# SBUF pools that wait tile by tile, a token quantizer on VectorE alone, and key tiles filled by ScalarE, in an eleven-block perceiver kernel

## The chip, the cores and the metric

The kernel runs on one core of one Trainium2 chip. A core has five engines with a queue of instructions each: TensorE (PE in the profile, with its weight loads as PEld), VectorE (DVE), ScalarE (ACT), GpSimd (POOL) and SyncE (SP), which here issues the DMA transfers. They run side by side and wait for one another through semaphores. The metric is the device time of one execution in microseconds (us); the median of several runs is compared.

## What is computed

The reference is a perceiver-like network of four layers on 2 batches of 256 tokens with 256 features (512 tokens in all), with a context of 4096 rows for each batch. Each layer has a cross attention to the context, a self attention and a feed-forward block. The block that most of the change lies in is layer 0's feed-forward, in which both products take quantized operands:

```
def act_quant(x):
    scale = 127.0 / clip(max(abs(x), axis=-1), 1e-05)
    return clip(round(x * scale), -128, 127) / scale
def weight_quant(w):
    scale = 1.0 / clip(mean(abs(w)), 1e-05)
    return clip(round(w * scale), -1, 1) / scale
def bit_linear(x, w):
    xq = x + stop_gradient(act_quant(x) - x)
    wq = w + stop_gradient(weight_quant(w) - w)
    return einsum('bsd,hd->bsh', xq, wq)
# block: layernorm -> bit_linear(w1) to 1024 features -> depthwise convolution
#        over 3 tokens -> silu -> bit_linear(w2) back to 256 -> + x
```

Each token has its own scale, the largest magnitude of its features. The value that enters the product is x + (quantized - x), in that order of operations.

## The kernel before

Activations stand in SBUF with features on the partitions: x is a tile of [128, 2, 512] (two halves of the features by 512 tokens), float32. The program is eleven blocks, one after the other: l0_xattn, l0_attn, l0_ffn together with l1_xattn, l1_attn, l1_ffn, l2_xattn, l2_attn, l2_ffn, l3_xattn, l3_attn, l3_ffn. In the profiled execution L0's cross attention fills about 40 to 700 us, L0_attn's attention 767 to 848, L0_ffn 850 to 954, L1's cross attention 970 to 1635.

A scheduler orders the instructions of most blocks; inside manual_schedule the named engines keep the order in which the program is written. Both large cross attentions (class ContextAttention) are written out by hand for PE, VectorE and ScalarE. The order of all other instructions is the same before and after the change.

Memory comes from pools that are opened and closed with the blocks. A pool that is opened over the bytes of closed ones must wait for those who used them. The argument reuse_waits says how: with "pool" (the default) all its tiles wait for every user of the closed pools whose bytes the new pool lands on; with "tile" each tile waits only for the users of earlier tiles on its own bytes. The pools of PSUM and of the small temporary tiles (banks, stage) have "tile" already; the SBUF pools of the blocks have the default.

L0_ffn runs inside the set-up of L1's cross attention: context_attention opens its pools xa and xa_ctx, the constructor of ContextAttention has POOL clear two xa_top tiles (L780) and fill fourteen key tiles xa_k of 128x512 with ones (L783), and then calls l0_ffn with the generator begin(3), which projects three sets of keys. l0_ffn advances it one step at a time (run(between, 1)), so PE's k_ps products (L1001) stand between its own. SP copies masks (key_masks) and dense keys into the filled key tiles.

The steps of L0_ffn, in order:

- Before it, L0_attn quantizes the weights: w1 on VectorE, w2 on POOL (quantize_weights, L522 to L526, two parts of 128x1024). Then x is complete (L312).
- norm: mean (PE), xc (VectorE L232), sq (ScalarE L233), var (PE), a table load and rstd (ScalarE L249, VectorE L250), rstd_ps (PE), h (VectorE L281).
- to_tokens transposes h into tok_ps (PE L563); two copies into hn, one on ScalarE and one on VectorE (L219).
- quantize_tokens(hn): the largest magnitude (L533), four operations on 128x4 for scale and inverse (L534 to L537), and for each of 4 groups of 128 tokens five operations: times the scale and rounded (L522), lower bound (L523), upper bound and rescaled (L524), minus src (L525), plus src (L526).
- from_tokens transposes back (feat_ps, PE L574), copies (L219), and w1's products follow (proj), the convolution (ScalarE L1237, VectorE L1240) and silu (ScalarE L1243).
- by_token for each of the 4 groups: eight transposes to hid_tok (PE L1254), a copy to tok (ScalarE L1258), quantize_tokens of 128x1024, with L525 on POOL and the rest on VectorE.
- For each group: eight transposes to feat_ps, two copies to hidq (L219, dealt to ScalarE and VectorE by the scheduler), and w2's products into l0f_out (PE, 16 products in 32 instructions).

Other places that the change touches: the value tiles xv of the cross attentions, set by eleven POOL memsets of 128x1148 (L1038) at their start, beside which VectorE makes the queries xa_q (L816, L818 or L820); the table loads ahead of the first exponential of a self attention (ScalarE L368 in L0_attn and L2_attn, L1439 in L1_attn and L3_attn); in L3_attn the memset of sa_v (POOL L1317) and the band mask (POOL L1848 and L1851, cast by VectorE L1863).

Of the kernel before, what the change touches and what calls it, by code (L numbers as in the profile page):

```python
# [19 lines left out]
F32 = mybir.dt.float32  # L20
# [3 lines left out]
ALU = mybir.AluOpType  # L24
# [46 lines left out]
class Net:  # L71
# [385 lines left out]
    def attend_to_context(self, a, x, q_bias, wq, wo, alive):  # L457
        tc = self.tc
        with self.stage():
            norm = self.center(self.halves(x))  # L460
            if not a.begun:
                a.beginning = a.begin(2)
                run(a.beginning, 1)
            a.take_queries(norm, wq, q_bias, alive)
        with (
            self.banks(mm=1, sc=3, acc=1),
            tc.tile_pool(name="xa_v", bufs=1) as vpool,
            tc.tile_pool(name="xa_p", bufs=1) as ppool,
            tc.tile_pool(name="focus", bufs=2) as fpool,
        ):  # L470
            a.attend(vpool, ppool, fpool)
        with self.stage():
            return a.give_back(x, wo)

    def context_constants(self):
# [8 lines left out]
        self.key_masks = self.tc.dram_tile([2, NR, KC], F32, name="key_masks")  # L484
        with self.banks(), self.tc.tile_pool(name="mask", bufs=1) as tmp:
            mi = tmp.tile([NR, KC], I32, name="mask_i", tag="mask_i")
# [29 lines left out]

    def quantize(self, work, out, src, scale, inverse, low, high, first, second, third):


        n = src.shape[-1]  # L520
        t = work.tile([P, 1024], F32, tag="quant", name="quant", bufs=2)[:, :n]
        first.tensor_scalar(t, src, scale, MAGIC, ALU.mult, ALU.add)  # L522
        first.tensor_scalar(t, t, MAGIC, low, ALU.subtract, ALU.max)  # L523
        first.tensor_scalar(t, t, high, inverse, ALU.min, ALU.mult)  # L524
        second.tensor_tensor(t, t, src, ALU.subtract)  # L525
        third.tensor_tensor(out, t, src, ALU.add)  # L526

    def quantize_tokens(self, work, out, src, rows, between=None):

# [6 lines left out]
        nc.vector.tensor_scalar_mul(scale, scale, 127.0)  # L536
        nc.vector.reciprocal(inverse, scale)  # L537
        for r in range(rows):
            of = scale[:, r : r + 1], inverse[:, r : r + 1]
            self.quantize(work, out[:, r, :], src[:, r, :], *of, -128.0, 127.0, nc.vector, between or nc.vector, nc.vector)  # L540

    def quantize_weights(self, work, w, total, n, engine):
# [9 lines left out]
        for at in range(0, 2048, 1024):  # L552
            part = w[:, at : at + 1024]
            self.quantize(work, part, part, scale, inverse, -1.0, 1.0, engine, engine, engine)

# [11 lines left out]

    def from_tokens(self, outs, src, n):

        for m in range(0, n, 4):  # L570
            k = min(4, n - m)
            ps = self.mm("feat_ps")
            for i in range(k):
                self.nc.tensor.transpose(ps[:, i * P : (i + 1) * P], src[:, (m + i) * P : (m + i + 1) * P], self.ident)  # L574
            self.copy(outs(m, k), ps[:, : k * P].rearrange("p (k t) -> p k t", k=k))
# [185 lines left out]
class ContextAttention:  # L761
# [11 lines left out]
    def __init__(self, net, layer, big, cpool, keys, values):  # L773
# [7 lines left out]
        self.key_tiles = [tile([P, KC], f"k{i}") for i in range(self.KEY_TILES)]  # L781
        for t in self.key_tiles:
            self.nc.gpsimd.memset(t, 1.0)  # L783
        self.begun, self.beginning = 0, iter(())
# [363 lines left out]
def l0_attn(net, x):  # L1148
# [8 lines left out]
    NCH = 8  # L1157
    with tc.tile_pool(name="l0a", bufs=1) as big, tc.tile_pool(name="l0a_w", bufs=2) as work:
        cos, sin = net.vec("rope_cos", big), net.vec("rope_sin", big)
# [58 lines left out]
def l0_ffn(net, x, between):  # L1218
# [4 lines left out]
    NCH = 8  # L1223
    with tc.tile_pool(name="l0f", bufs=1) as big, tc.tile_pool(name="l0f_w", bufs=2) as work:
# [26 lines left out]
        def by_token(t):  # L1251
# [36 lines left out]
def small_attention(net, x, wq, wk, wv, wo, scale, qb=None, kb=None, vb=None, ob=None, window=None):  # L1288

    by_program = {mybir.EngineType.PE, mybir.EngineType.DVE, mybir.EngineType.Activation}  # L1290
    with net.tc.manual_schedule(engines=by_program):
        with net.tc.tile_pool(name="sa", bufs=1) as big, net.tc.tile_pool(name="sa_w", bufs=1) as work:
            a = SmallAttention(net, big, work, scale, vb, window)
# [180 lines left out]
def l1_ffn(net, x):  # L1474
# [7 lines left out]
    hc = [h[:, d, :] for d in range(ND)]  # L1482
    with tc.tile_pool(name="l1f", bufs=1) as big, tc.tile_pool(name="l1f_w", bufs=2) as work:
        tile3 = lambda name: big.tile([P, NT, E], F32, name=name, tag=name)
# [83 lines left out]
def l2_xattn(net, x):  # L1568
# [5 lines left out]
    with (  # L1574
        tc.manual_schedule(engines={mybir.EngineType.PE}),
        tc.tile_pool(name="l2x", bufs=1) as big,
        tc.tile_pool(name="l2x_t", bufs=5) as cpool,
        tc.tile_pool(name="l2x_n", bufs=4) as npool,
    ):
# [100 lines left out]
def l2_attn(net, x):  # L1680
# [10 lines left out]
    NCH = 8  # L1691
    with tc.tile_pool(name="l2a", bufs=1) as big, tc.tile_pool(name="l2a_w", bufs=2) as work:
        mask = mask_tile(net, big, "causal", (1, 0))
# [46 lines left out]
def l2_ffn(net, x):  # L1740
# [8 lines left out]
    h = net.norm(x)  # L1749
    with tc.tile_pool(name="l2f", bufs=1) as big:  # L1750
        mixed = [big.tile([P, ND, T], F32, name=f"mix{i}", tag=f"mix{i}") for i in range(2)]
# [24 lines left out]
def l3_xattn(net, x):  # L1776
# [3 lines left out]
    net.measure(norm)  # L1780
    with tc.tile_pool(name="l3x", bufs=1) as big, tc.tile_pool(name="l3x_w", bufs=2) as work:

# [94 lines left out]
def l3_ffn(net, x):  # L1877
    nc, tc = net.nc, net.tc
    E, NCH, HC = 64, 4, 2
    y = net.norm(x)  # L1880
    with tc.tile_pool(name="l3f", bufs=1) as big, tc.tile_pool(name="l3f_w", bufs=2) as work:
        mask = mask_tile(net, big, "window", (1, 0), (-1, P))
# [319 lines left out]
```

## Time and profile before

| | before |
|---|---|
| median of 3 runs | 2561.95 us (2557.09 to 2562.78) |
| the profiled execution's own time | 2563.84 us |
| its span, first to last instruction | 2562.1 us |
| mean granted TensorE clock | 0.953 |
| busy PE / DVE / ACT / POOL | 2343.6 / 1558.8 / 1054.6 / 355.6 us |

The profile is of one execution. A row of its timeline gives the start (us from the span's start), the busy time, the engine, the line of the program, the operation, the tiles written and read with their shapes, and how many instructions are put together; in brackets stands how long the engine had been idle and what released it. L219 and L180 are the lines of helpers (a copy, a product), so these rows are told apart by their tiles. The chain that ended last follows the execution back from its last instruction, at each step to what released it. In the stretches of L0_ffn the engines were busy as follows:

| stretch, us | PE | DVE | ACT | POOL | granted clock |
|---|---|---|---|---|---|
| 838 to 876 | 23.00 | 11.64 | 3.36 | 35.51 | 0.79 |
| 876 to 886 | 0.00 | 9.62 | 0.59 | 6.92 | 0.50 |
| 886 to 913 | 21.40 | 15.17 | 13.77 | 0.00 | 0.85 |
| 913 to 955 | 31.37 | 27.67 | 8.38 | 9.49 | 0.84 |

### The profile page before, as it was taken

What the parts mean: (1) busy time and instruction counts of PE and PEld (TensorE: products, weight loads), DVE (VectorE), ACT (ScalarE), POOL (GpSimd) and SP (SyncE); (2) the same over time, 40 slices, a digit from 0 to 9 for tenths busy, and PEclk for the clock granted to TensorE, in tenths of its full rate; (3) what the DMA queues carried; (4) which work ended last, traced back from release to release, by engine and by line L of the source; (5) the groups of instructions that cost most, each with busy time, mean ns of one, the idle gap of its engine ahead of it and who ended that gap; (6) DMA issues with size and microseconds to landing.
All of it is one profiled execution on the core that took longest, in us unless ns stands there. A gap on an engine that the chain in (4) does not pass through costs nothing.

```text
span 2562.1 us, 42559 instructions
## 1 busy us (share of the span) xinstructions
PE 2343.6 (91%) x17006; PEld 1247.1 (49%) x17014; DVE 1558.8 (61%) x2702; ACT 1054.6 (41%) x1830; POOL 355.6 (14%) x523
## 2 busy tenths in 40 slices
PE   7999999999998579999999999989999996789998
PEld 3454545544544354544555544554448453345453
DVE  4968897779546468888878878243331254335252
ACT  2455555555616132555555555431131252223141
POOL 3000010000034612100011000000020031003030
PEclk9999999999989789999999999988999897898989
DMA  5432223231010133232222220202222100000100
GB/s 191 137 97 80 93 88 94 71 107 43 10 55 17 47 107 108 91 95 95 94 88 82 83 76 26 81 14 61 87 89 88 42 18 14 33 21 12 56 12 21
DMA packets 97797, 174.40 MB, mean 68 GB/s; under 512 B 15120, under 2 KB 63888, under 8 KB 96704
## 3 DMA queue, kind: packets, MB, share of 16 engines
q1 hardware_dynamic: 97600, 171.68, 20.7%
q8 instruction: 135, 2.21, 0.4%
q14 instruction: 62, 0.51, 0.1%
HBM read 154.25 MB, written 0.59 MB: 60 GB/s over the span
## 4 chain that ended last, share of the span: by engine, by line
PE 79%; DVE 10%; ACT 5%; issue 3%; POOL 2%; DMA 1%; SPq 0%; ACTq 0%; DVEq 0%; POOLq 0%
PE s L1080 11%; PE s L1104 10%; PE attn_acc L1128 9%; PE v_ps L180 6%; PE proj L180 6%; PE k_ps L1001 4%; DVE mx L1088 3%; PE kc_sum L180 2%; PE expert L180 2%; PE s L180 2%; PE c_acc L1666 2%; PE f_ps L180 2%; PE ffn_ps L180 2%; PE s L1402 2%; PE o L411 1%
## 5 line engine op out<-in xcount | busy, mean ns | idle before, releaser
L1088 DVE TENSOR_REDUCE mx<-s 128x2 f32<-128x1024 f32 x512 | 603.5, 1220 | 206.3 <-PE s L1080 203.6
L1114 ACT ACTIVATE p<-s 128x1024 f32<-128x1024 f32 x512 | 496.3, 1021 | 237.9 <-PE s L1104 235.8
L1104 PE MATMUL s<-xa_q,xa_k 32*128 32x256 f32 x4096 | 339.0, 403 | 22.9 <-DVE mx L1088 20.8
L1080 PE MATMUL s<-xa_k,xa_q 32*128 32x512 f32 x2048 | 345.3, 639 | 7.6 <-ACT p L1114 3.6
L1104 PEld LDWEIGHTS s<-xa_q,xa_k 32*128 32x128 f32 x4096 | 211.8, 184 | 160.5 <-issue 98.5
L1128 PE MATMUL attn_acc<-p,xv 128*32 128x256 f32 x4096 | 277.1, 387 | 0.9 <-ACT p L1114 0.9
L1080 PEld LDWEIGHTS s<-xa_k,xa_q 32*128 32x128 f32 x2048 | 116.4, 183 | 128.9 <-issue 58.7
L654 DVE TENSOR_TENSOR ge<-fy 128x960 bf16<-128x960 f32 (+14 forms) x240 | 172.9, 720 | 6.2
L1128 PEld LDWEIGHTS attn_acc<-p,xv 128*32 128x32 f32 x4096 | 107.5, 109 | 132.2 <-issue 85.5
L611 POOL TENSOR_TENSOR fy<-fy,low 128x256 f32<-128x256 f32 x64 | 50.4, 787 | 793.1 <-ACT low L610 793.1
L656 DVE TENSOR_TENSOR rank<-rank,ge 128x960 bf16<-128x960 bf16 (+14 forms) x240 | 111.4, 464 | 6.0
L658 DVE TENSOR_TENSOR rank<-rank,ge 128x960 bf16<-128x960 bf16 (+14 forms) x240 | 105.6, 440 | 2.7
L387 POOL TENSOR_SCALAR p<-p,r 128x128 f32<-128x128 f32 (+1 forms) x192 | 82.7, 444 | 140.2 <-DVE r L383 80.0
L1048 ACT COPY xv<-v_ps 128x512 f32<-128x512 f32 x64 | 37.6, 588 | 142.8 <-PE v_ps L180 133.0
L368 ACT ACTIVATE p<-p,top 128x256 f32<-128x256 f32 (+1 forms) x128 | 57.1, 447 | 42.7 <-DVE top L356 40.2
L180 PE MATMUL f_ps<-f_wk,f_ctx 128*128 128x256 f32 x256 | 70.0, 401 | 1.2 <-ACT low L610 1.2
L1001 PE MATMUL k_ps<-ctx_k,w_L0x_wq 128*64 128x512 f32 x256 | 65.1, 615 | 2.6 <-DMA ctx_k<-in_ctxT 2.2
L1666 PE MATMUL c_acc<-pT,ctx_n 128*128 128x256 f32 x256 | 63.1, 392 | 4.2 <-ACT pT L1639 3.0
L180 PEld LDWEIGHTS f_ps<-f_wk,f_ctx 128*128 128x128 f32 x256 | 44.1, 189 | 46.8 <-issue 27.3
L233 ACT ACTIVATE sq<-xc 128x512 f32<-128x512 f32 x24 | 14.7, 630 | 125.8 <-DVE xc L232 125.8
L180 PE MATMUL v_ps<-w_L0x_wv,ctx_v 128*128 128x256 f32 x256 | 63.8, 392 | 0.8 <-ACT k_dense L1014 0.8
L180 PE MATMUL kc_sum<-f_tok,fy 128*128 128x257 f32 x256 | 64.2, 393 | 0.0
(458 smaller groups left out, 3365.1 us busy)
## 6 DMA issues: line engine op xcount, KB each, us to landing
ctx_k<-in_ctxT SPq DMA_DIRECT2D x128, 512.0 KB
ctx_v<-in_ctxT SPq DMA_DIRECT2D x64, 256.0 KB
xa_k<-k_dense SPq DMA_DIRECT2D x512, 32.0 KB
f_ctx<-in_ctxT SPq DMA_DIRECT2D x32, 256.0 KB
f_tok<-in_ctx SPq DMA_DIRECT2D x16, 512.0 KB
ctxT<-in_ctxT SPq DMA_DIRECT2D x16, 512.0 KB
ctx_n<-in_ctx SPq DMA_DIRECT2D x16, 512.0 KB
xa_k<-key_masks SPq DMA_DIRECT2D x128, 8.0 KB
```

Of the source, the lines that this page charges most:

```text
L180: self.nc.tensor.matmul(out, lhsT=lhsT, rhs=rhs, start=i == 0, stop=i == len(pairs) - 1)
L387: nc.gpsimd.tensor_scalar(p[:, j, :nk], p[:, j, :nk], r[:, j : j + 1], 1.0, ALU.mult, ALU.mult)
L654: nc.vector.tensor_tensor(ge[:, :, :n], w[:, :, :n], w[:, :, P - n :], ALU.is_ge)
L656: nc.vector.tensor_tensor(rank[:, :, P - n :], rank[:, :, P - n :], ge[:, :, :n], ALU.add)
L658: nc.vector.tensor_tensor(rank[:, :, :n], rank[:, :, :n], ge[:, :, :n], ALU.subtract)
L1001: nc.tensor.matmul(ps[i * HR : (i + 1) * HR, :], lhsT=self.wk[:, d, c * HR : (c + 1) * HR], rhs=ctx[:, d, :], start=d == 0, stop=d == ND - 1,)
L1080: nc.tensor.matmul(pairs[i // 2][:, i % 2, :], lhsT=self.q[u][rows, qt * P : (qt + 1) * P], rhs=k[rows, :], start=True, stop=True,)
L1088: nc.vector.tensor_reduce(mx[:, qt, 2 * i : 2 * i + 2, kc], sc, AX.X, ALU.max)
L1104: nc.tensor.matmul(pairs[i // 2][:, i % 2, kk * S : (kk + 1) * S], lhsT=k[rows, at], rhs=self.q[u][rows, :], start=True, stop=True,)
L1114: nc.scalar.activation(p, sc, AF.Exp, scale=DH**-0.5)
L1128: nc.tensor.matmul(self.acc[i * HP : (i + 1) * HP, :S], lhsT=v[:, 2 * k2 + kk, at : at + HP], rhs=ps[i // 2][:, i % 2, kk * S : (kk + 1) * S],
L1666: nc.tensor.matmul(accs[m], lhsT=of[:, (k + i) % (KC // P), m * P : (m + 1) * P], rhs=pT[:, i, :], start=k + i == 0, stop=k + i == KT - 1,)
```

## The change

It has three parts.

1. Every SBUF pool of the blocks gets reuse_waits="tile" (on sixteen lines; one of them is shown).
2. The token quantizer runs on VectorE alone. For the 1024-wide tokens of L0_ffn it stops ahead of the last addition and returns the difference (quant); from_tokens then makes the sum on PE: two products with the identity, of tok and of the difference, accumulate into feat_ps in place of one transpose. The quant tile has four buffers for two. Both hidq copies that VectorE did go to ScalarE.
3. L1's fourteen key tiles are filled by ScalarE, which copies a column of ones, as a first step of begin; l0_ffn runs that step behind the quantization of hn in program order, and the scheduler puts five of the copies ahead of sq, one between the two sq, one ahead of rstd's table load and seven ahead of the hn copy. L0's key tiles stay with POOL.

Counted in instructions: POOL loses 14 memsets and 4 subtractions; ScalarE gains 14 + 2 copies; VectorE gains 4 subtractions and loses 4 additions and 2 copies; PE gets 64 products for 32 transposes.

The waits that change with the pools, as far as the prediction speaks of them: the hn copies no longer wait for the end of w2's quantization on POOL, the second L522 of the tokens waits for it instead; most xv memsets wait for sq and PE's last query projection, no longer for VectorE's last L816, and only the tenth waits for VectorE; the table loads at L368 and at L1497 (L1_ffn) no longer wait for VectorE's data, while the one at L1439 in L3_attn waits for PE's s; the memset of sa_v in L3_attn waits for an earlier copy on VectorE (yT) in place of the last y.

```diff
-        with tc.tile_pool(name="xa", bufs=1) as big, tc.tile_pool(name="xa_ctx", bufs=2) as cpool:
+        with tc.tile_pool(name="xa", bufs=1, reuse_waits="tile") as big, tc.tile_pool(name="xa_ctx", bufs=2, reuse_waits="tile") as cpool:
...
-    def quantize(self, work, out, src, scale, inverse, low, high, first, second, third):
+    def quantize(self, work, out, src, scale, inverse, low, high, engine):
...
-        t = work.tile([P, 1024], F32, tag="quant", name="quant", bufs=2)[:, :n]
-        first.tensor_scalar(t, src, scale, MAGIC, ALU.mult, ALU.add)
-        first.tensor_scalar(t, t, MAGIC, low, ALU.subtract, ALU.max)
-        first.tensor_scalar(t, t, high, inverse, ALU.min, ALU.mult)
-        second.tensor_tensor(t, t, src, ALU.subtract)
-        third.tensor_tensor(out, t, src, ALU.add)
+        t = work.tile([P, 1024], F32, tag="quant", name="quant", bufs=4)[:, :n]
+        engine.tensor_scalar(t, src, scale, MAGIC, ALU.mult, ALU.add)
+        engine.tensor_scalar(t, t, MAGIC, low, ALU.subtract, ALU.max)
+        engine.tensor_scalar(t, t, high, inverse, ALU.min, ALU.mult)
+        engine.tensor_tensor(t, t, src, ALU.subtract)
+        if out is not None:
+            engine.tensor_tensor(out, t, src, ALU.add)
+        return t
...
-    def from_tokens(self, outs, src, n):
+    def from_tokens(self, outs, src, n, more=None):
...
-                self.nc.tensor.transpose(ps[:, i * P : (i + 1) * P], src[:, (m + i) * P : (m + i + 1) * P], self.ident)
+                at, to = slice((m + i) * P, (m + i + 1) * P), ps[:, i * P : (i + 1) * P]
+                if more is None:
+                    self.nc.tensor.transpose(to, src[:, at], self.ident)
+                else:
+                    self.matmuls(to, [(of[:, at], self.ident) for of in (src, more)])
...
-        for t in self.key_tiles:
-            self.nc.gpsimd.memset(t, 1.0)
+        if layer == 0:
+            for t in self.key_tiles:
+                self.nc.gpsimd.memset(t, 1.0)
...
         self.begun = n
+        if self.layer > 0:
+            for t in self.key_tiles:
+                self.nc.scalar.copy(t, self.net.ones[:, 0:1].to_broadcast([P, KC]))
+            yield
         for j in range(n):
...
         net.quantize_tokens(work, hn, hn, NT)
+        run(between, 1)
         hq = big.tile([P, ND, T], F32, name="hq", tag="hq")
...
-            net.quantize_tokens(work, tok, tok, 1, nc.gpsimd)
-            toks.append(tok)
+            toks.append((tok[:, 0, :], *net.quantize_tokens(work, None, tok, 1)))
...
-            net.from_tokens(lambda m, k: hidq[:, m : m + k, at], toks[t][:, 0, :], NCH)
+            tok, more = toks[t]
+            net.from_tokens(lambda m, k: hidq[:, m : m + k, at], tok, NCH, more)
```

More of the change, by code (lines that the diff above doesn't have):

```diff
@@ L466, in attend_to_context @@
             self.banks(mm=1, sc=3, acc=1),
-            tc.tile_pool(name="xa_v", bufs=1) as vpool,
-            tc.tile_pool(name="xa_p", bufs=1) as ppool,
-            tc.tile_pool(name="focus", bufs=2) as fpool,
+            tc.tile_pool(name="xa_v", bufs=1, reuse_waits="tile") as vpool,
+            tc.tile_pool(name="xa_p", bufs=1, reuse_waits="tile") as ppool,
+            tc.tile_pool(name="focus", bufs=2, reuse_waits="tile") as fpool,
         ):
@@ L484, in context_constants @@
         self.key_masks = self.tc.dram_tile([2, NR, KC], F32, name="key_masks")
-        with self.banks(), self.tc.tile_pool(name="mask", bufs=1) as tmp:
+        with self.banks(), self.tc.tile_pool(name="mask", bufs=1, reuse_waits="tile") as tmp:
             mi = tmp.tile([NR, KC], I32, name="mask_i", tag="mask_i")
@@ L514, in context_constants, with quantize_tokens @@
             nc.vector.tensor_scalar_min(self.alive, ps[:, :NB], 1.0)
-    def quantize(self, work, out, src, scale, inverse, low, high, first, second, third):
+    def quantize(self, work, out, src, scale, inverse, low, high, engine):
         n = src.shape[-1]
-        t = work.tile([P, 1024], F32, tag="quant", name="quant", bufs=2)[:, :n]
-        first.tensor_scalar(t, src, scale, MAGIC, ALU.mult, ALU.add)
-        first.tensor_scalar(t, t, MAGIC, low, ALU.subtract, ALU.max)
-        first.tensor_scalar(t, t, high, inverse, ALU.min, ALU.mult)
-        second.tensor_tensor(t, t, src, ALU.subtract)
-        third.tensor_tensor(out, t, src, ALU.add)
-    def quantize_tokens(self, work, out, src, rows, between=None):
+        t = work.tile([P, 1024], F32, tag="quant", name="quant", bufs=4)[:, :n]
[6 more added lines that the diff above has]
+        return t
+    def quantize_tokens(self, work, out, src, rows):
         nc = self.nc
@@ L537, in quantize_tokens @@
         nc.vector.reciprocal(inverse, scale)
+        more = []
         for r in range(rows):
             of = scale[:, r : r + 1], inverse[:, r : r + 1]
-            self.quantize(work, out[:, r, :], src[:, r, :], *of, -128.0, 127.0, nc.vector, between or nc.vector, nc.vector)
+            to = None if out is None else out[:, r, :]
+            more.append(self.quantize(work, to, src[:, r, :], *of, -128.0, 127.0, nc.vector))
+        return more
     def quantize_weights(self, work, w, total, n, engine):
@@ L553, in quantize_weights @@
             part = w[:, at : at + 1024]
-            self.quantize(work, part, part, scale, inverse, -1.0, 1.0, engine, engine, engine)
+            self.quantize(work, part, part, scale, inverse, -1.0, 1.0, engine)
     def to_tokens(self, out, src):
@@ L1157, in l0_attn @@
     NCH = 8
-    with tc.tile_pool(name="l0a", bufs=1) as big, tc.tile_pool(name="l0a_w", bufs=2) as work:
+    with tc.tile_pool(name="l0a", bufs=1, reuse_waits="tile") as big, tc.tile_pool(name="l0a_w", bufs=2, reuse_waits="tile") as work:
         cos, sin = net.vec("rope_cos", big), net.vec("rope_sin", big)
@@ L1223, in l0_ffn @@
     NCH = 8
-    with tc.tile_pool(name="l0f", bufs=1) as big, tc.tile_pool(name="l0f_w", bufs=2) as work:
+    with tc.tile_pool(name="l0f", bufs=1, reuse_waits="tile") as big, tc.tile_pool(name="l0f_w", bufs=2, reuse_waits="tile") as work:
         h = net.norm(x)
@@ L1291, in small_attention @@
     with net.tc.manual_schedule(engines=by_program):
-        with net.tc.tile_pool(name="sa", bufs=1) as big, net.tc.tile_pool(name="sa_w", bufs=1) as work:
+        with net.tc.tile_pool(name="sa", bufs=1, reuse_waits="tile") as big, net.tc.tile_pool(name="sa_w", bufs=1, reuse_waits="tile") as work:
             a = SmallAttention(net, big, work, scale, vb, window)
@@ L1482, in l1_ffn @@
     hc = [h[:, d, :] for d in range(ND)]
-    with tc.tile_pool(name="l1f", bufs=1) as big, tc.tile_pool(name="l1f_w", bufs=2) as work:
+    with tc.tile_pool(name="l1f", bufs=1, reuse_waits="tile") as big, tc.tile_pool(name="l1f_w", bufs=2, reuse_waits="tile") as work:
         tile3 = lambda name: big.tile([P, NT, E], F32, name=name, tag=name)
@@ L1575, in l2_xattn @@
         tc.manual_schedule(engines={mybir.EngineType.PE}),
-        tc.tile_pool(name="l2x", bufs=1) as big,
-        tc.tile_pool(name="l2x_t", bufs=5) as cpool,
-        tc.tile_pool(name="l2x_n", bufs=4) as npool,
+        tc.tile_pool(name="l2x", bufs=1, reuse_waits="tile") as big,
+        tc.tile_pool(name="l2x_t", bufs=5, reuse_waits="tile") as cpool,
+        tc.tile_pool(name="l2x_n", bufs=4, reuse_waits="tile") as npool,
     ):
@@ L1691, in l2_attn @@
     NCH = 8
-    with tc.tile_pool(name="l2a", bufs=1) as big, tc.tile_pool(name="l2a_w", bufs=2) as work:
+    with tc.tile_pool(name="l2a", bufs=1, reuse_waits="tile") as big, tc.tile_pool(name="l2a_w", bufs=2, reuse_waits="tile") as work:
         mask = mask_tile(net, big, "causal", (1, 0))
@@ L1749, in l2_ffn @@
     h = net.norm(x)
-    with tc.tile_pool(name="l2f", bufs=1) as big:
+    with tc.tile_pool(name="l2f", bufs=1, reuse_waits="tile") as big:
         mixed = [big.tile([P, ND, T], F32, name=f"mix{i}", tag=f"mix{i}") for i in range(2)]
@@ L1780, in l3_xattn @@
     net.measure(norm)
-    with tc.tile_pool(name="l3x", bufs=1) as big, tc.tile_pool(name="l3x_w", bufs=2) as work:
+    with tc.tile_pool(name="l3x", bufs=1, reuse_waits="tile") as big, tc.tile_pool(name="l3x_w", bufs=2, reuse_waits="tile") as work:
         kvs = []
@@ L1880, in l3_ffn @@
     y = net.norm(x)
-    with tc.tile_pool(name="l3f", bufs=1) as big, tc.tile_pool(name="l3f_w", bufs=2) as work:
+    with tc.tile_pool(name="l3f", bufs=1, reuse_waits="tile") as big, tc.tile_pool(name="l3f_w", bufs=2, reuse_waits="tile") as work:
         mask = mask_tile(net, big, "window", (1, 0), (-1, P))
```

## The prediction

> **What bounds the kernel now.** I read the page first (shares, then the chain that ended last), then the timeline of each engine around every place that the change touches, then the chain of that stretch.
>
> ```profile
> PE 2343.6 (91%) x17006; PEld 1247.1 (49%) x17014; DVE 1558.8 (61%) x2702; ACT 1054.6 (41%) x1830; POOL 355.6 (14%) x523
> PE 79%; DVE 10%; ACT 5%; issue 3%; POOL 2%; DMA 1%; SPq 0%; ACTq 0%; DVEq 0%; POOLq 0%
> ```
>
> TensorE (PE) carries 79% of the chain, and the two hand-planned cross attentions make most of that. An edit outside them is worth something only where the chain leaves PE. One such place is L0_ffn, 850 to 954 us. Its head:
>
> ```profile
> 876.03 0.36 POOL L780 MEMSET xa_top<- 128x128 f32 x2
> 876.32 6.60 POOL L783 MEMSET xa_k<- 128x512 f32 x14
> ...
> 876.14 0.69 DVE L219 COPY hn<-tok_ps 128x512 f32<-128x512 f32 x1 [12.97 <-POOL w_L0f_w L526]
> 876.94 1.22 DVE L533 TENSOR_REDUCE scale<-hn 128x4 f32<-128x1024 f32 x1
> 878.19 4.75 DVE L534 TENSOR_SCALAR scale<-scale 128x4 f32<-128x4 f32 x1
> 882.98 0.18 DVE L535 RECIPROCAL scale<-scale 128x4 f32<-128x4 f32 x1
> ...
> 886.11 1.09 PE L574 MATMUL feat_ps<-ident,hn 128*128 128x128 f32 x4 [21.13 <-issue]
> ```
>
> The reader is to see three things. PE stands still for 21.13 us. VectorE's copy into hn waits 12.97 us for POOL's last step of w2's quantization, which hn doesn't use (the tokens, tok_ps, were ready near 865); it is the pool's wait. And a 128x4 operation takes 4.75 us where its neighbours take 0.18: it ends at 882.94, with POOL's fourteen memsets (876.32 + 6.60 = 882.92). The end of the block:
>
> ```profile
> 919.31 2.34 POOL L525 TENSOR_TENSOR quant<-quant,tok 128x1024 f32<-128x1024 f32 x1 [36.39 <-DVE scale L535]
> ...
> 919.51 2.69 DVE L522 TENSOR_SCALAR quant<-tok,scale 128x1024 f32<-128x1024 f32 x1
> ...
> 924.51 1.97 PE L574 MATMUL feat_ps<-ident,tok 128*128 128x128 f32 x8 [6.63 <-DVE tok L526]
> 926.30 4.72 PE L180 MATMUL l0f_out<-hidq,w_L0f_w 128*128 128x128 f32 x32
> 931.30 1.07 PE L574 MATMUL feat_ps<-ident,tok 128*128 128x128 f32 x8 [0.28 <-DVE tok L526]
> 932.61 3.84 PE L180 MATMUL l0f_out<-hidq,w_L0f_w 128*128 128x128 f32 x32 [0.24 <-ACT hidq L219]
> ...
> 942.57 6.72 PE L180 MATMUL l0f_out<-hidq,w_L0f_w 128*128 128x128 f32 x32 [2.89 <-DVE hidq L219]
> ```
>
> Here VectorE sets the pace (a token each 6.7 us), held by POOL's subtraction; PE waits and then runs cold: the same 32 instructions take 3.84 warm, 4.72 and 6.72 after waits.
>
> **The change, part by part.** The profiled execution took 2563.84 us (span 2562.1 and 1.7 around it), 1.89 above the median of the runs, 2561.95. I sum against 2563.84 and take the difference off the median. 0.2% is 5.1 us.
>
> *Head of L0_ffn.* ScalarE gets fourteen 128x512 copies; its like in this trace takes 0.53 to 0.59 us. Five stand ahead of sq and start when x is ready (853.46): 2.7 us, until 856.2, where sq begins now (856.26). One stands between the two sq, one ahead of rstd's table load: rstd, h and tok_ps come 1.1 us later, about 866. The last seven take 3.8 us beside PE's and VectorE's norm and are done near 864.6, so the hn copies follow at 866 to 867. All of it is hidden by w2's quantization on POOL, which still ends at 876.03: the second L522 of the tokens now waits for it, since its quant tile lies on w2's. So that wait moves from the hn copies to the second L522, which stood at 883.73 and can stand at 876.2: 7.5 us. Behind it on VectorE is only the rest of hn's quantization; PE's feat_ps waits for that. If the four small operations can't get in while POOL is busy (as at 878.19) they run at 876.4 to 877.1, and 6.4 are left. I take **-7.0**. The mask and key transfers on SP now wait for ScalarE's copies (864.6 against 882.9); their keys are used at 972, so nothing comes of it.
>
> Here a rule of the Trainium skill stands against the row. The page "SBUF — State Buffer" (section "Who interferes with whom") says that an operation of VectorE and one of GpSimd exclude each other on the shared port pair for one whole instruction. By that, L534 would have lost one memset (0.47 each) and the memsets would be worth 0.5. The row shows nine or ten of them lost, so I count 4.6 of the 7.0 to them. The rule counts again below.
>
> *Tokens.* Removed: POOL's four L525 (2.35 each), VectorE's four L526 (1.21) and two hidq copies (to ScalarE). Added: four L525 on VectorE, 1.21 each as L526. Without POOL, VectorE's token costs 1.13+0.65+0.60+0.67+1.13 and 0.58 of small ones = 4.8 us; the first is ready 6.5 us after its first reduction (10.5 until now). Each of 32 transposes becomes two products. A product of this shape costs 3.84/16 = 0.24, a transpose 1.07/8 = 0.134: PE gets 4x(3.84-1.07) = 11.1 us more, and becomes the bound with 3.84+0.24+3.84 = 7.9 a token. Shifted by 7.0 the first reduction is at 907.0, the first quant at 913.5, and the end at 913.5 + 4x7.92 + 1.94 (k_ps between) = 947.1, warm. Unchanged it would be 954.25 - 7.0 = 947.25. So it is even when warm. Cold: PE waits some 2.8 us ahead of the first token (k_ps ends at 908.9 + 1.9). The page "TensorE: Matmul & The Clock Gate" (section "What's actually happening") has the clock halved only after an idle window of about 3.4 us: by that nothing or little is lost; by the row of 942.57 a wait of 2.89 cost 6.72-3.84 = 2.9, by that of 924.51 a wait of 6.63 cost 1.8. I take **+1.3**, ends -0.1 and +2.8.
>
> *Pools elsewhere.* Most of the moved waits end no chain: another operand is later. The exceptions are table loads that carried the data's wait.
>
> ```profile
> 768.75 1.28 ACT L368 ACT_TABLE_LOAD   x1 [0.90 <-DVE top L352]
> ...
> 2037.91 1.28 ACT L368 ACT_TABLE_LOAD   x1 [28.77 <-DMA w_L2f_wr<-in_L2f_wr]
> ...
> 2218.62 1.28 ACT L1439 ACT_TABLE_LOAD   x1
> ...
> 2228.54 1.94 ACT L1439 ACTIVATE p<-s 128x1024 f32<-128x1024 f32 x2 [8.63 <-PE s L1402]
> ...
> 2189.72 0.43 DVE L1863 CAST band<-band_f 128x512 bf16<-128x512 f32 x1 [3.06 <-POOL band_f L1851]
> ```
>
> In L0_attn the load loses its wait for top, runs behind the last v copy (767.85 to 769.1) and the first exponential comes 0.9 earlier; the loop behind is a chain of latencies with PE waiting for p, so **-0.9** (between 0 and -0.9). In L2_attn likewise, 2039.20 to 2038.0: **-1.2** (0 to -1.2). L1_ffn's load (1748.14) is freed too, but PE has no gap there: 0. In L3_attn it is the other way: the load now takes the wait for PE's s, and the exponential starts 1.28 later: **+1.3** (0 to +1.3). There too POOL's sa_v memset no longer waits for PE's last proj, so band is cast before x is ready and xc (2190.06) starts after mean, 2188.8: **-1.1** (0 to -1.1). For L1_attn, L1_ffn and L2x the released memsets and tables sit under PE's work: 0; without that cover each is a memset, about 1 us.
>
> *Starts of both cross attentions.* POOL's eleven xv memsets may start some 1.2 us earlier.
>
> ```profile
> 33.09 1.31 DVE L818 TENSOR_SCALAR xa_q<-xa_q,vectors 128x256 f32<-128x256 f32 x1
> ...
> 33.20 11.11 POOL L1038 MEMSET xv<- 128x1148 f32 x11 [17.82 <-DVE xa_q L816]
> ```
>
> Now the last query operation waits for one memset (1.31 for 0.35). Started earlier, two will wait for one each, and the last ends where it does: 0.
>
> Sum: -7.0+1.3-0.9-1.2+1.3-1.1 = **-7.6**: 2556.2 of the profiled execution, 2554.4 on the median. With all bounds -10.7 to -2.3.
>
> **Rivals.** (1) *The tokens eat it* (0.18): PE cold for its whole first block, small operations starved, table loads worth nothing: -6.4+2.8+1.3 = -2.3, up to -5; 2557 to 2559.7. For it: 11.1 us of added PE work. Against: the first quant is 4 us earlier. (2) *VectorE starved by xv memsets* (0.10), the slower end: the last query operation at 32.4 and at 971.2 meets memsets that already run, and gets in only when nine have run (the tenth waits for VectorE), as at 878.19, not at the first change. 9x1.01 from 32.0 ends at 41.1 against 34.4, 6.7 late, and 6.9 at 973.3; L0's start is partly waiting for DMA, so 5 to 6.7 there: 12 to 13.6 lost, net +4.4 to +6.0, 2566 to 2568. It decides from the third memset on: below that the sum stays negative. For it: row 878.19. Against: row 33.09, where it got in at the first change, and the page's rule of one instruction. (3) *The pools do nothing* (0.04): the wait for w2 is on the chain either way, only the memsets' 4.6 go: -4.6+1.3 = -3, 2559. That needs quant's wait to stand ahead of the reduction.
>
> **How the numbers follow.** The likeliest, 0.68, gives 2554.4 with 2551.3 to 2559.7. Faster by more than 5.1 us needs -5.1 of the -7.6: most of 0.68 and a little of rival 1: 0.68. Within 0.2%: rivals 1 and 3, the weak end of the likeliest, half of rival 2: 0.23. Slower: the rest of rival 2 and what I don't see, 0.09. The range runs from 2550.5 (all bounds, and a little) to 2561.5, which leaves out rival 2.
>
> **What would show it.** Right: hn copies near 866, no L534 over 1 us at 877, the second L522 at 876 waiting for POOL, PE's idle before feat_ps 14 rather than 21 us; feat_ps 3.8 a token, no wait over 0.5 us between tokens; exponentials at 769 and 2038 minus the shift, a table load ahead of 2229 in L3_attn. Wrong: an xa_q operation of 5 us or more at 32 or 965; hn copies still at 876; an end of l0f_out after 951.

## The result, and the profile after

The changed kernel takes 2552.8 us (median of 20 runs, 2545.43 to 2555.93) against 2558.06 (20 runs, 2550.32 to 2567.34) of the kernel before, measured in turn. The ratio is 0.9973, 95% interval 0.9963 to 0.9984: 6.9 us faster (9.5 to 4.1); the medians alone differ by 5.3, the means by 7.0. The forecast was 7.6 us. The profiled execution took 2554.6 us, its span 2552.9, the mean granted clock 0.956.

The page of the changed kernel, busy time by engine and the chain that ended last:

```profile
PE 2353.5 (92%) x17110; PEld 1256.4 (49%) x17110; DVE 1551.8 (61%) x2700; ACT 1063.2 (42%) x1846; POOL 342.1 (13%) x505
PE 79%; DVE 9%; ACT 5%; issue 3%; POOL 2%; DMA 1%; SPq 0%; ACTq 0%; DVEq 0%; POOLq 0%
```

PE has 9.9 us more to do and the kernel is faster: the added products took the place of waits. The head of L0_ffn in the timeline of the changed kernel (VectorE, then PE, then POOL; L536 to L539 are the former L534 to L537, L527 the former L526, L568 and L582 the former L563 and L574):

```profile
865.68 0.69 DVE L219 COPY hn<-tok_ps 128x512 f32<-128x512 f32 x1 [0.99 <-PE tok_ps L568]
...
868.40 0.44 DVE L536 TENSOR_SCALAR scale<-scale 128x4 f32<-128x4 f32 x1
868.88 0.18 DVE L537 RECIPROCAL scale<-scale 128x4 f32<-128x4 f32 x1
869.09 2.05 DVE L538 TENSOR_SCALAR scale<-scale 128x4 f32<-128x4 f32 x1
871.17 0.18 DVE L539 RECIPROCAL inverse<-scale 128x4 f32<-128x4 f32 x1
871.27 2.29 DVE L522 TENSOR_SCALAR quant<-hn,scale 128x256 f32<-128x256 f32 x1
875.79 0.40 DVE L522 TENSOR_SCALAR quant<-hn,scale 128x256 f32<-128x256 f32 x1 [2.23 <-POOL w_L0f_w L527]
...
878.26 1.09 PE L582 MATMUL feat_ps<-ident,hn 128*128 128x128 f32 x4 [11.77 <-DVE hn L527]
...
866.47 4.64 POOL L525 TENSOR_TENSOR quant<-quant,w_L0f_w 128x1024 f32<-128x1024 f32 x2
871.07 4.68 POOL L527 TENSOR_TENSOR w_L0f_w<-quant,w_L0f_w 128x1024 f32<-128x1024 f32 x2
```

The copy into hn waits 0.99 us for its data instead of 12.97 for POOL, the wait for w2 now stands at the second L522, and feat_ps starts 7.9 us earlier. Three of VectorE's operations (0.44, 2.05, 2.29 us) were each held to the end of the POOL operation that ran, and then went through. The tokens:

```profile
910.76 0.49 PE L180 MATMUL feat_ps<-ident,tok 128*128 128x128 f32 x2
913.41 0.49 PE L180 MATMUL feat_ps<-ident,quant 128*128 128x128 f32 x2 [2.16 <-DVE scale L538]
...
916.86 3.85 PE L180 MATMUL l0f_out<-hidq,w_L0f_w 128*128 128x128 f32 x32
...
924.12 3.78 PE L180 MATMUL l0f_out<-hidq,w_L0f_w 128*128 128x128 f32 x32
927.83 1.94 PE L1016 MATMUL k_ps<-ctx_k,w_L1x_wq 128*64 128x512 f32 x8
...
940.57 3.78 PE L180 MATMUL l0f_out<-hidq,w_L0f_w 128*128 128x128 f32 x32
```

PE works from 913.41 to 944.3 without a pause and without a cold stretch; the granted clock between 913 and 955 us is 1.00 (0.84 before). It is the bound here now: VectorE is done with its last token at 926.4. The table loads of L0_attn, L2_attn and L3_attn, and the band mask of L3_attn:

```profile
768.08 1.28 ACT L368 ACT_TABLE_LOAD   x1
769.37 0.47 ACT L368 ACTIVATE p<-scores,top 128x256 f32<-128x256 f32 x1
...
1999.57 1.28 ACT L368 ACT_TABLE_LOAD   x1
2028.29 0.40 ACT L368 ACTIVATE p<-p,top 128x128 f32<-128x128 f32 x1 [27.43 <-DVE top L356]
...
2177.11 0.43 DVE L1879 CAST band<-band_f 128x512 bf16<-128x512 f32 x1 [3.08 <-POOL band_f L1867]
2177.45 1.28 DVE L232 TENSOR_TENSOR xc<-x,mean 128x512 f32<-128x512 f32 x2
...
2215.95 1.28 ACT L1455 ACT_TABLE_LOAD   x1 [11.49 <-PE s L1418]
2217.24 1.94 ACT L1455 ACTIVATE p<-s 128x1024 f32<-128x1024 f32 x2
```

The first two loads run ahead of their data now, the third behind it, and xc still follows the cast of band.

To see where the difference lies, I cut each profile at the ends of VectorE's last addition into x of each block, and L0_ffn also at the first reduction of a token. The row of before gives each stretch in us; the others give the difference to it. The last column runs to VectorE's last instruction; blocks that are not shown are in it. e11 is the kernel before, profiled a second time.

```
                    L0x    L0a  L0f head  L0f tokens    L1x    L2x    L2a    L3a    L3f   whole
before           709.54 143.92     60.52       40.99 688.57 136.39 125.28 104.16 265.82  2558.3
e11 before again   4.40  -1.14      0.36       -1.46  -2.00  -1.39  -4.55  -0.07  -0.08    -6.3
changed            3.38  -3.78     -6.64       -2.84   0.37  -0.04  -2.49   2.29   0.44    -9.2
e1 only pools      4.96  -5.47     -2.96       -1.30   2.68   0.07  -2.40   2.28   0.44    -2.4
e2 only fill      -0.04  -1.95     -4.29       -1.48  -2.07  -1.38  -4.24  -0.18  -0.13   -16.2
e3 only tokens    -0.73   0.11      0.04       -1.28  -3.33  -1.23  -4.38  -0.07  -0.08   -10.8
e4 no fill         3.02  -0.59      0.04       -2.84   4.68  -0.03  -2.46   2.29   0.43     3.8
e5 fill, tokens    1.80  -0.29     -4.04       -1.28  -1.85  -1.23  -4.27  -0.08  -0.08    -8.8
e6 preload         0.76  -1.98     -6.94       -1.22  -1.82  -0.02  -2.49   3.17  -0.14   -11.3
e7 xv pool        -1.92  -0.75     -6.63       -2.85   1.07   0.02  -2.45   4.48  -1.41   -11.8
e8 sum on DVE      1.28  -2.41     -6.65       -7.84   0.55   0.10  -2.42   1.15  -1.82   -17.8
e9 head pools      3.77  -3.60     -7.25       -9.42  -1.06  -1.24  -4.27  -0.03  -0.05   -20.8
e10 fill, sum      4.87  -3.61     -4.23       -9.27  -1.05   0.11   1.41   2.41  -4.17   -12.0
e12 chosen pools   2.39  -0.55     -6.90       -9.22   0.35  -1.23  -6.57   0.16   0.33   -18.3
```

The row of e11 is the scale for the rest: without any change, the cross attentions, L2_attn and the whole move by 1 to 6 us from one profile to the next. In the column of L0_ffn's head the kernels fall into groups by what was edited there. In that of the tokens they do too, but kernels with the same tokens stand 1.6 us apart (-2.84 and -1.28; e3 below shows why). In the others they hardly do (L3_attn's +2.3 comes with the pools' part, and in e10 without it).

### The profile page after: what moved, and what is told of

It is laid out like the page before. It is cut to its first block, busy times and chain, and to the rows that moved or that the text cites. A ratio compares the mean times of both kernels' runs of the same rounds, so it can differ in the third digit from the quotient of the medians.

```text
span 2552.9 us, 42753 instructions
## 1 busy us (share of the span) xinstructions
PE 2353.5 (92%) x17110; PEld 1256.4 (49%) x17110; DVE 1551.8 (61%) x2700; ACT 1063.2 (42%) x1846; POOL 342.1 (13%) x505
## 4 chain that ended last, share of the span: by engine, by line
PE 79%; DVE 9%; ACT 5%; issue 3%; POOL 2%; DMA 1%; SPq 0%; ACTq 0%; DVEq 0%; POOLq 0%
PE s L1095 11%; PE s L1119 11%; PE attn_acc L1143 9%; PE v_ps L180 6%; PE proj L180 6%; PE k_ps L1016 4%; DVE mx L1103 3%; PE kc_sum L180 2%; PE expert L180 2%; PE s L180 2%; PE c_acc L1682 2%; PE f_ps L180 2%; PE ffn_ps L180 2%; PE s L1418 2%; PE o L411 1%
## 5 line engine op out<-in xcount | busy, mean ns | idle before, releaser
L368 ACT ACTIVATE p<-p,top 128x256 f32<-128x256 f32 (+1 forms) x128 | 57.1, 447 | 68.2 <-DVE top L356 65.7
L180 PE MATMUL v_ps<-w_L0x_wv,ctx_v 128*128 128x256 f32 x256 | 63.8, 392 | 0.8 <-ACT k_dense L1029 0.8
L180 PE MATMUL v_ps<-w_L1x_wv,ctx_v 128*128 128x256 f32 x256 | 63.8, 392 | 0.0
```

The source lines that it names most:

```text
L180: self.nc.tensor.matmul(out, lhsT=lhsT, rhs=rhs, start=i == 0, stop=i == len(pairs) - 1)
```

## The experiments

**The parts alone, and the fill undone.** e1 is the kernel before with the pools' part, e2 with ScalarE's fill, e3 with the token quantizer; e4 is the changed kernel with POOL's fill:

```diff
e1, on before (sixteen lines like this)
-    with tc.tile_pool(name="l0f", bufs=1) as big, tc.tile_pool(name="l0f_w", bufs=2) as work:
+    with tc.tile_pool(name="l0f", bufs=1, reuse_waits="tile") as big, tc.tile_pool(name="l0f_w", bufs=2, reuse_waits="tile") as work:
e2, on before
-        for t in self.key_tiles:
-            self.nc.gpsimd.memset(t, 1.0)
+        if layer == 0:
+            for t in self.key_tiles:
+                self.nc.gpsimd.memset(t, 1.0)
...
+        if self.layer > 0:
+            for t in self.key_tiles:
+                self.nc.scalar.copy(t, self.net.ones[:, 0:1].to_broadcast([P, KC]))
+            yield
...
+        run(between, 1)
e4, on the changed kernel: the same, reversed
```

e3 is the changed kernel with both of these taken back.

> The kernel before with the pools' waits alone (reuse_waits="tile" on all SBUF pools); POOL still fills the key tiles and takes the tokens' subtraction. The hn copies should come near 865 instead of 876 and the second L522 at 876.2, but POOL's fourteen memsets then run from 876.3 to 882.9 beside the quantization of hn. Theory S (VectorE gets no turn between memsets that follow one another, as at 878.19 before): one operation of the quantization is held until 882.9, feat_ps starts at 885 to 886, the head gains under 1 us, and the whole kernel only what the pools give elsewhere, -2 to -3 us. Theory L (one instruction at a time): every operation loses at most one memset of 0.47, feat_ps starts at 879 to 881, the kernel gains 7 to 9 us. Both: the first exponentials of L0_attn and L2_attn 0.9 and 1.2 earlier, that of L3_attn 1.3 or more later.

> The kernel before with the fourteen key tiles filled by ScalarE, nothing else. The hn copies still wait for w2 on POOL (876.1). Theory M (the 4.75 us of the 128x4 operation at 878.19 were the memsets): it takes 0.2, feat_ps starts near 881.5, and the kernel is 4.6 us faster. Rival (the memsets cost one instruction, 0.5 us, and the rest of the 4.75 had another cause): feat_ps not before 885, the kernel within 1 us of before.

> The kernel before with the new token quantizer and the sum by products on PE alone; pools and POOL's memsets as before. Theory W (PE stays warm through the four tokens, a token costs 7.2 us with the 16 products at 0.22 each, as in the changed kernel's profile): from the first reduction of the tokens to the end of l0f_out it takes 37.2 us against 40.3 before, the kernel is 2.5 to 3 us faster. Rival C (the forecast's term: products 0.24 each, a wait for hidq in each token, a cold first block): 41.6 us, the kernel 1.3 us slower.

> The changed kernel with the key tiles filled by POOL again (pools and tokens as changed). Theory S: feat_ps at 884 to 886 and not at 878.3, 6 to 7 us slower than the changed kernel, 3 to 5 faster than before. Theory L: feat_ps at 879 to 881, 1 to 3 us slower than the changed kernel. If the parts simply add, e1 + e3 = this one.

Measured: e1 1.000 (0.9986 to 1.0013), e2 0.9971 (0.9958 to 0.9984), e3 0.9973 (0.9962 to 0.9983), e4 0.9997 (0.9983 to 1.0011). The head in e2: hn still waits for POOL, and the stall is gone.

```profile
874.15 0.69 DVE L219 COPY hn<-tok_ps 128x512 f32<-128x512 f32 x1 [12.22 <-POOL w_L0f_w L526]
...
876.21 0.17 DVE L534 TENSOR_SCALAR scale<-scale 128x4 f32<-128x4 f32 x1
```

The 4.75 us were the memsets (theory M): the head is 4.3 shorter. (The runs give e2 7.4 us; the 3 beyond the head are not explained.) In e1 and e4 the memsets are there, and the quantization of hn meets them. The same wait of VectorE on the same string of memsets ends in two ways, e1 first:

```profile
871.17 4.92 DVE L522 TENSOR_SCALAR quant<-hn,scale 128x256 f32<-128x256 f32 x2
876.02 1.30 DVE L523 TENSOR_SCALAR quant<-quant 128x256 f32<-128x256 f32 x2
877.24 1.29 DVE L524 TENSOR_SCALAR quant<-quant,inverse 128x256 f32<-128x256 f32 x2
...
879.79 1.36 DVE L522 TENSOR_SCALAR quant<-hn,scale 128x256 f32<-128x256 f32 x2
...
875.89 8.15 POOL L783 MEMSET xa_k<- 128x512 f32 x14
```

Then e4:

```profile
878.62 6.94 DVE L522 TENSOR_SCALAR quant<-hn,scale 128x256 f32<-128x256 f32 x1 [4.53 <-POOL w_L0f_w L527]
885.49 0.47 DVE L523 TENSOR_SCALAR quant<-quant 128x256 f32<-128x256 f32 x2
...
878.53 0.34 POOL L790 MEMSET xa_top<- 128x128 f32 x2
878.82 6.60 POOL L793 MEMSET xa_k<- 128x512 f32 x14
```

In e1 VectorE was already waiting behind w2's quantization when the memsets began. It takes turns with them: two operations take 1.30 us instead of 0.48, the string of memsets stretches from 6.60 to 8.15 us, and the head still gains 3.0. In e4 the L522 came up behind POOL's string (878.62 against 878.53) and got nothing until it ended (885.42): the whole gain of the pools in the head is gone (0.04). But coming late is not what decides: e1's L522 at 879.79 also came up while the memsets ran, after L525 and L526 had run beside them without loss (0.74 and 0.75 for two), and it lost one memset. Why the two kernels differ stays open. Both theories, S and L, describe one of the two runs each. So pools and fill belong together: pools alone 3.0 or 0, fill alone 4.3, both 6.6.

e3's tokens come out 1.3 shorter than before, where the changed kernel's are 2.84 shorter. PE's rows of e3 show the difference:

```profile
919.88 0.49 PE L180 MATMUL feat_ps<-ident,quant 128*128 128x128 f32 x2 [2.16 <-DVE scale L538]
...
920.43 0.39 PE L180 MATMUL feat_ps<-ident,quant 128*128 128x128 f32 x2
...
920.95 0.63 PE L180 MATMUL feat_ps<-ident,quant 128*128 128x128 f32 x2
```

PE waits 2.16 us for the first difference, as in the changed kernel, and soon after it resumes, two instructions take 0.63 us instead of 0.39, until 923.9. The granted clock is 0.50 between 922 and 924 us (1.00 in the changed kernel); PE runs at half clock for about 3.4 us, which costs 1.6. The same wait and such a stretch stand in e5 and e6 below; in e4 and e7, as in the changed kernel, the same wait cost nothing. So theory W holds for the products (3.8 and 0.39), and rival C's cold first block comes and goes.

The old tokens have such stretches too, two of 6.8 us in the profile of before, one of 6.8 and one of 3.4 in e11. Against e11 (-1.46) the new tokens bring nothing in e3, e5 and e6, and 1.4 in the changed kernel, e4 and e7. The runs give e3 6.9 us (4.5 by plain means), more than its block shows; where the rest lies I could not find.

**Without the pools' part; a table loaded early; the xv pool; the sum on VectorE.** e5 is the changed kernel with the pools as before. The others are the changed kernel with one edit each:

```diff
e6, in SmallAttention.attend
         n = len(self.UNITS)
+        ready = self.net.sm(1, name="ready", tag="ready")
+        self.nc.scalar.activation(ready, self.net.eps5, AF.Exp)
e7
-            tc.tile_pool(name="xa_v", bufs=1, reuse_waits="tile") as vpool,
+            tc.tile_pool(name="xa_v", bufs=1) as vpool,
e8
-            toks.append((tok[:, 0, :], *net.quantize_tokens(work, None, tok, 1)))
+            net.quantize_tokens(work, tok, tok, 1)
+            toks.append((tok[:, 0, :], None))
```

> The changed kernel without its pools' part: all SBUF pools wait for the whole closed pool as before; ScalarE fills the key tiles, the tokens are quantized the new way. Theory P (the pools cost as much as the rest brings: e3 and e4 differ by the pools and stand at 0.9973 and 0.9997): the two parts add, -4.8 in the head and about -3 at the tokens, ratio 0.994 to 0.996, faster than the changed kernel (0.9973) by 4 to 8 us; no loss at the start of L0's cross attention (+2 to +3 in every profile with the pools) nor in L3_attn (+5 from rstd to the block's end). Rival F (the forecast: the pools bring 2.4 in the head and 1.9 elsewhere): slower than the changed kernel by about 4 us, 0.9985 to 0.999.

> The changed kernel with one exponential of a single constant, written ahead of the first scores of L1_attn and L3_attn (as the cross attentions have it): the table is loaded then, and the first exponential of L3_attn waits for nothing but its data. Theory T (the table load behind PE's s is the loss in L3_attn): from rstd to the end of L3_attn's loop the kernel loses 0 to 1 us against before instead of 5, and is 3 to 5 us faster than the changed kernel. Forecast's size: 1.3 us. Rival (L3_attn's loss is PE's clock alone): no more than 0.5 us.

> The changed kernel with the pool of the value tiles (xa_v) alone back on whole-pool waits, so POOL's xv memsets start behind VectorE's last L816 as before. Theory X (memsets that start 1.2 us earlier hold two query operations, PE's second score waits and PE falls to its slow clock): the start of L0's cross attention stands within 0.5 us of before at 45 us instead of 1.7 to 2 later, L1's likewise; the kernel 2 to 5 us faster than the changed one. Forecast: 0.

> The changed kernel with VectorE making the sum too (L527 for the tokens, 1.13 more on VectorE for each) and from_tokens transposing as before: no products for the sum. VectorE's token costs 5.9 us, PE's 1.07+0.8+3.8 = 5.7. Theory V (the added 11 us of PE are the bound of this stretch, VectorE alone is the gain): l0f_out ends 5 to 7.5 us earlier than in the changed kernel (29.8 to 32.3 us after the first reduction instead of 37.3). Rival W (waits between tokens drop PE to its slow clock, as before the change): within 2 us of the changed kernel.

Measured: e5 0.9974 (0.9962 to 0.9985), e6 0.9959 (0.9946 to 0.9972), e7 0.9963 (0.9949 to 0.9977), e8 0.9955 (0.9941 to 0.9969).

e5 stands where the changed kernel stands. Neither expectation held: the parts do not add to 0.995, and the pools bring nothing either. They bring 2.6 in the head (-6.64 against -4.04); that this isn't seen in the runs is within what these tell apart, and in the profiles e5 makes it up behind L0_ffn (L2x, L2a and L3a, 5.3 shorter together than in the changed kernel).

e6 did what its edit says, the first exponential of L3_attn follows PE's s without a load (2217.42), but L3_attn is no shorter (+3.17 against +2.29), since PE was cold in the block: its last 16 kq_ps instructions took 10.18 us, against 8.80 in the changed kernel and 8.58 in e5. Theory T is neither shown nor refuted; the intervals of e6 and of the changed kernel overlap. In e7 the start of L0's cross attention is as theory X has it: PE's first scores wait 1.39 us again instead of 1.87, and the k_ps products behind them take 1.94 instead of 3.38 (the rows are shown below, where the forecast's term is judged). But the runs of e7 and of the changed kernel are not told apart either, so what that is worth in the whole isn't shown.

e8 is clear in its own block. PE's rows:

```profile
913.94 1.97 PE L582 MATMUL feat_ps<-ident,tok 128*128 128x128 f32 x8 [3.83 <-DVE tok L527]
915.82 5.93 PE L180 MATMUL l0f_out<-hidq,w_L0f_w 128*128 128x128 f32 x32
921.59 1.04 PE L582 MATMUL feat_ps<-ident,tok 128*128 128x128 f32 x8
922.87 3.84 PE L180 MATMUL l0f_out<-hidq,w_L0f_w 128*128 128x128 f32 x32 [0.24 <-ACT hidq L219]
...
934.79 3.84 PE L180 MATMUL l0f_out<-hidq,w_L0f_w 128*128 128x128 f32 x32 [0.24 <-ACT hidq L219]
```

The first token is late and cold (a wait of 3.83, then 5.93 for 3.84), the other three flow. The tokens take 7.8 us less than before, 5.0 less than in the changed kernel, which had no cold stretch (theory V). In e9, e10 and e12 below, with the same wait of 3.83 or 3.84, the cold stretch cost 1.4 to 1.7 us instead of 3.0, and the tokens take 9.2 to 9.4 less than before. What the quantizer gains is POOL's subtraction moved to VectorE; the sum by products gives 5 us of it back, or 8.0 by e5 and e10, which differ by this edit alone.

**What the profiles point to.** e9 is the kernel before with ScalarE's fill, VectorE's quantizer including the sum, and tile-by-tile waits for the two lines of pools that the head needs (xa and xa_ctx, l0f and l0f_w). e10 has no pools' part at all, e12 has the pools of L0_attn and L2_attn beside those of e9. e11 is before, unchanged. The edits are those shown above.

> The kernel before with the key tiles filled by ScalarE, the tokens quantized by VectorE alone (sum included, no products for it), and tile-by-tile waits for the pools of L0_ffn and of L1's keys (xa, l0f and their partners) alone; all other SBUF pools as before. If the head needs these pools and nothing else: head -6.6, tokens -7.8 as in e8, and no +2.3 in L3_attn: 1 to 4 us faster than e8 (ratio to before 0.9955 there), 0.994 to 0.995. If the other pools bring something (the forecast: 1.9), it is slower than e8 by that.

> The same without any change to the pools. The head should stand at -4.3 (as e2 and e5, the hn copies at 876), the tokens near -7.8; so 2.4 us slower than e9 if the pools' wait for w2 is worth what the profiles of e5 and the changed kernel differ by in the head (-4.0 against -6.6), and no slower if that is lost again.

> The kernel before, once more. It shows what one profile's blocks differ by without a change. If PE's slow clock comes and goes by chance, L2_attn's value products (15.88 us in the profile before and in all profiles with the pools' part, 13.12 in those without it) and L0's and L1's cross attentions move by 1 to 4 us here too, and the ratio is 1.000. If those differences belong to the pools, L2_attn stands at 125.3 again and the cross attentions within 1 us.

> As e9, and tile-by-tile waits also for the pools of L0_attn and L2_attn, whose table loads then run ahead of their data. By the profiles the first exponential comes 0.7 us earlier in L0_attn and 1.0 in L2_attn: 1.7 us faster than e9, if the blocks behind don't give it back.

Measured: e9 0.9923 (0.9904 to 0.9942), e10 0.994 (0.9921 to 0.996), e11 1.0012 (1.0001 to 1.0022), e12 0.9929 (0.991 to 0.9948).

e9 beats both kernels: 2541.0 us (6 runs), 0.77% under before, and its interval lies below that of the changed kernel. The head is 7.25 and the tokens 9.4 us shorter than in the profile of before, 16.7 of the 19.7 that the ratio stands for. e10's head is 4.23 shorter, as expected; the 3 us that the pools bring there (-7.25 against -4.23) are about what lies between e9 and e10, though their intervals overlap. e12 is not told from e9.

e11 shows two things. An identical kernel comes out at 1.0012, so differences of 0.1 to 0.2% between two kernels of this size are not to be read. And L2_attn's value products (PE's timeline, the profile of before first, then e11):

```profile
1984.53 1.12 PE L180 MATMUL v_ps<-w_L2a_wv,xc 128*128 128x512 f32 x2
1987.58 15.88 PE L180 MATMUL v_ps<-w_L2a_wv,xc 128*128 128x512 f32 x30
```

```profile
1983.10 1.13 PE L180 MATMUL v_ps<-w_L2a_wv,xc 128*128 128x512 f32 x2
1985.55 13.12 PE L180 MATMUL v_ps<-w_L2a_wv,xc 128*128 128x512 f32 x30
```

The same 30 instructions take 15.88 or 13.12 us in the same program. The expectation's first case holds: what had looked like a mark of the pools' part (15.88 with it, 13.12 without) comes without it too, here and in e10 (15.98). Whether the pools make it likelier is not settled: all six profiles with their whole part, or all of it but xa_v, have the long case, and two of the eight others.

## Why the prediction was right, and where it was not

**The head, -7.0: right.** The block's column says -6.6 in the changed kernel, and -6.6 to -6.9 in e6, e7 and e8 as well. ScalarE's copies were hidden, as reckoned: five took 2.69 us from 853.09, the last ended at 864.6, and the hn copies followed at 865.7 and 866.5. The wait went to the second L522 (875.79). The 4.6 of it that I put down to the memsets are e2's 4.3.

**The rule of one instruction: each side had half of it.** I held the row of 878.19 against the page "SBUF — State Buffer" (section "Who interferes with whom"), and e2 says that the row was the price of this string. But beside w2's quantization (868 to 874), beside the xv memsets and in e1, VectorE lost one POOL instruction each time, as the page says (for a VectorE instruction in a two-port mode; which mode these had, no trace shows). It lost what was left of the whole string in before, e3 and e4 (and in e11, 4.77). There VectorE's operation came up after the string of 128x512 memsets had begun, but so did e1's at 879.79, which lost one. What decides is not shown.

**The tokens, +1.3: too dear.** In the changed kernel they took 2.84 us less than before and 1.4 less than in e11; in e3, e5 and e6 about as long as in e11. The mis-sized term is PE's: the 7.92 a token measured about 7.2, since 32 instructions of the sum take 3.45 to 3.7 and not 3.84, and the wait for hidq (0.24) is covered by the next products. Four times the difference of 0.7 makes up the 2.7 between the forecast from the first reduction to the end of l0f_out (947.1 - 907.0 = 40.1) and the 37.4 measured.

The part of the term for a cold first block was 1.4, and the runs give 0 or 1.6 for the same wait of 2.16 us: 0 in the changed kernel, e4 and e7, 1.6 in e3, e5 and e6. So the page "TensorE: Matmul & The Clock Gate" (section "What's actually happening"), with the clock halved only after an idle window of about 3.4 us, was no sure guide here: in e3 an idle stretch of 2.16 was enough. The row of 942.57 was none either. The wait of 2.89 that cost 2.9 before cost 1.4 in e11 (5.25 us for 3.84, after 2.90), and 3.83 us cost 3.0 in e8 (1.97 + 5.93 against 1.04 + 3.84), 1.4 in e9. The stretches at half clock were 3.4 or 6.8 us long in each case that was read (e3, e9, before, e8, e11), and the page lets its window run free of the program; that would make the price of a short wait a matter of chance, but no run here shows what sets it off.

**The table loads: right in mechanism and size where they can be read.** In L0_attn the exponential comes 0.9 earlier against the v copies ahead of it (769.37 for 770.04, with the copies at 767.48 for 767.26). In L2_attn it starts 1.0 behind PE's scores (2027.25) and 2.4 before (2036.84): 1.3 gained. In L3_attn it waits 1.29 for the load. What the blocks made of it can't be read: L0_attn and L2_attn moved by 1.1 and 4.6 without a change (e11).

**The band mask, -1.1: wrong.** The step "no longer waits for PE's last proj" was misread: the wait that went was for VectorE's last y, and POOL's sa_v memset still waits for proj. xc follows the cast at 2177.45 as it did at 2190.06. The term is 0.

**Starts of the cross attentions, 0: right for VectorE, not for PE.** Rival 2 is refuted by the timeline of the changed kernel: two query operations lose one memset each, and the last ends at 34.31, before at 34.40.

```profile
32.34 0.83 DVE L833 TENSOR_SCALAR xa_q<-xa_q,vectors 128x256 f32<-128x256 f32 x1
33.09 0.41 DVE L831 TENSOR_TENSOR xa_q<-proj,wide 128x256 f32<-128x256 f32 x1
33.53 0.78 DVE L833 TENSOR_SCALAR xa_q<-xa_q,vectors 128x256 f32<-128x256 f32 x1
```

But PE's first scores start when the operation before the last is done, and that one is 0.4 us later. PE's rows, before first, then changed:

```profile
33.26 1.14 PE L1080 MATMUL s<-xa_k,xa_q 32*128 32x512 f32 x8 [1.39 <-issue]
34.33 1.94 PE L1001 MATMUL k_ps<-ctx_k,w_L0x_wq 128*64 128x512 f32 x8
```

```profile
33.70 1.35 PE L1095 MATMUL s<-xa_k,xa_q 32*128 32x512 f32 x8 [1.87 <-POOL xv L1053]
34.98 3.38 PE L1016 MATMUL k_ps<-ctx_k,w_L0x_wq 128*64 128x512 f32 x8
```

The wait is 1.86 or 1.87 in all five profiles with tile-by-tile waits for xa_v (changed, e1, e4, e6, e8) and 1.39 in the nine without. In three of the five (changed, e4, e8) PE then runs at half clock, and k_ps takes 2.9 to 3.4 us for 1.94. So the pools cost 0.5 us at this start and about 2 where the clock falls; how much of it lasts to the block's end can't be read, since L0x moves by 4.4 without a change.

So the sum of -7.6 came near 6.9 with a share of luck. L0_ffn alone is 9.5 us shorter in the changed kernel's profile (8.4 against e11), where the forecast had 5.7; the 1.9 that it had elsewhere did not come, and something was lost there. The terms that were wrong are the tokens, by 1.1 to 4.1, and the other way the band, by 1.1, and the starts. (The lower end of the bounds, -10.7, is -10.3 with the ends that the terms give.)

What stays open is the pools' part outside L0_ffn. By the runs it costs 6 us between e3 and e4 and 8 between e9 and e8 (of which L0_ffn's columns hold 2.2), and nothing between e5 and the changed kernel. The heads of e3 and e4 are equal, so it is not there. Two losses were seen, L3_attn's late load (1.3) and the start of L0's cross attention (0.5 to 2). The table points to more: L2x, L2a and L3a sum to between -1.2 and +2.1 in the six profiles with the pools' part, and to between -7.6 and -5.5 in six of the eight others. Before (0) and e10 (+3.9) stand high without it, so this is a place to look and not a cause.

## What to carry to other kernels

When a short wait is taken off the critical path, look at what is to run there next: here the operations that the pools freed ran into a string of short memsets on GpSimd and kept 3.0 us of the gain or none, and only the fill on a third engine made it safe. Before an engine that is 79% of the chain is given work that another could do, sum the stretch by engine: the addition by products cost 5 to 8 us more than the addition on VectorE (e8, and e10 against e5). And profile the unchanged kernel twice before blocks are compared: what differs between those two is no evidence.

## What the runs showed that was not expected

A VectorE operation that came up behind a string of 128x512 memsets on GpSimd waited for all that was left of it: 4.75 us (before), 4.76 (e3), 6.94 (e4). In e1 VectorE took turns with the same string (1.30 for two), even with an operation that came up in its middle (879.79), and between 128x1148 memsets it got in at the next change (0.83, 0.78). PE's stretches at half clock come and go in an unchanged program, 2.8 us in one group of 30 products, and after the same short wait: 2.16 us cost 0 or 1.6. Among the 20 runs of the changed kernel the fastest has the highest granted clock (2545.43 us at 0.961) and the slowest one of the lowest (2555.93 at 0.956); how much of the scatter between profiles these stretches make was not summed.
